# Every 68th quad of edge tiles: its node rows fetched by SyncE, one DMA per edge

## The chip, the core and the metric

The kernel runs on one core of a Trainium2 chip. The core has five instruction streams that run side by side and meet only at semaphores: TensorE (PE; its weight loads are PEld), VectorE (DVE), ScalarE (ACT), GpSimd (POOL) and SyncE (SP). Sixteen DMA engines move data between the chip's memory and the on-chip buffers; SP, ACT and POOL issue the transfers. The metric is the device time of one execution in microseconds, median of several runs; lower is better.

## What is computed

A message-passing layer of a graph network with residual and layer norm. There are 12500 nodes with 160 features (64 scalars `s` and 32 vectors `v` of three components) and 400000 edges, sorted by their destination.

```
h_s = s @ lin1_ws * a / sqrt(64)                 # per node
h_v = v @ lin1_wv * a / sqrt(32)
hid = silu(edge_scalars @ fc_w1 / sqrt(64))      # per edge
w1..w5 = split(hid @ fc_w2 / sqrt(64))
es, ev = h_s[edge_src], h_v[edge_src]            # the gather: one row of 160 floats per edge
messages = products of w1..w5, es, ev and edge_attr
agg  = segment_sum(messages, edge_dst)           # per node
out  = layernorm(x + gate(sc(s, v) + lin2(agg)))
```

## The kernel before

**Stages.** First, the node rows `h_s, h_v` are computed and written to a table `h_tab` in memory, 12500 rows of 160 floats (640 bytes). Then the edges run through a long loop; here almost all the time goes. Node windows that have all their edges are finished inside the loop, the last ones after it.

**The loop.** 128 edges are a tile, four tiles a quad; 3125 tiles make 782 steps of one quad (the last is smaller). The loop is unrolled in the program (`for n, (c, i, tiles) in enumerate(steps)`, line 819). A step:

- `fetch(n + 4)` (line 689): if the step four ahead begins a new chunk of 24 tiles (six steps), SP loads the chunk's edge scalars `es` (`load_chunk`, line 196, two DMAs of 384 KB, two buffers); each 72 tiles (18 steps) SP loads their source indices `idx` and edge attributes `eat` (`ahead`, lines 152 and 153).
- `gather(deep, ...)` (line 448): POOL issues four indirect DMAs, one per tile, each fetching 128 rows of `h_tab` by `idx` into `hg`. The pool `deep` has four buffers of `hg`, so POOL may run up to four quads ahead of the consumer.
- `weights` (line 465): PE forms the edge weights `pw` from `hid`.
- `products` (lines 475 and 483): DVE multiplies `pw` and `hg` to `pr`. This is where a quad's gathered rows are read.
- `select_quad`, `sum_up` (lines 537, 544): a one-hot matrix, scaled by the edge attributes, sums `pr` by destination on PE, two steps later.
- `hide(n + 2)`: PE and ACT compute `hid` for the step two ahead from `es` (lines 443, 445).
- now and then: `output` (second linear maps, register loads of window positions on DVE, line 764, and additions to `acc`), `finish` (a group of 512 nodes: load of `x`, line 592, normalisation, store of the result, line 644), `self_connection` (loads at lines 714 and 716).

**Order.** For PE, DVE, ACT and POOL the order of instructions in the loop is the one written in the program (`manual_schedule`, line 812). SP is not in that list: a scheduler places SP's transfers.

Of the kernel before, what the change touches and what calls it, by code (L numbers as in the profile page):

```python
# [10 lines left out]
F32 = mybir.dt.float32  # L11
I32 = mybir.dt.int32
I16 = mybir.dt.int16
BF16 = mybir.dt.bfloat16
AF = mybir.ActivationFunctionType
OP = mybir.AluOpType
AX = mybir.AxisListType
ENG = mybir.EngineType
PSUM = bass.MemoryType.PSUM

P = 128
# [3 lines left out]
D = S + V3  # L25
# [6 lines left out]
Q = 4  # L32
# [2 lines left out]
CT = 2 * SIDE  # L35
AHEAD = 3 * CT
NF = 4

MARGIN = 128
NO = 16  # L40
# [13 lines left out]
def gnn_kernel(  # L54
# [21 lines left out]
    nc = tc.nc  # L76
    N = x.shape[0]
# [3 lines left out]
    GT = src.shape[2]  # L81
# [7 lines left out]
    h_tab = dram.tile([N, D], F32, name="h_tab")  # L89
# [7 lines left out]
        engines={ENG.PE, ENG.DVE, ENG.Activation, ENG.Pool, ENG.SP}))  # L97
# [33 lines left out]
    steps = []  # L131
# [10 lines left out]
    def ahead(t):  # L142
        a0 = t // AHEAD * AHEAD
        if a0 not in aheads:
            n = min(AHEAD, TT - a0)
            idx = loads.tile([P, AHEAD], I32, name="idx")
            eat = loads.tile([P, AHEAD, 4], F32, name="eat")
            k = 0
            while k < n:
                g, u = divmod(a0 + k, GT)  # L150
                m = min(n - k, GT - u)
                nc.sync.dma_start(idx[:, k:k + m], src[g][:, u:u + m])
                nc.sync.dma_start(eat[:, k:k + m].rearrange("p t k -> p (t k)"),
                                  ea[g].rearrange("p t k -> p (t k)")[:, 4 * u:4 * (u + m)])
                k += m
            aheads[a0] = a0, idx, eat
        return aheads[a0]

    def index(t):
        a0, idx, _ = ahead(t)  # L160
        return idx[:, t - a0:t - a0 + 1]
# [26 lines left out]
    def load_chunk(c, queue=nc.sync):  # L188
        if c in ess:
            return  # L190
        t0, halves = chunks[c]
        es = ess[c] = loads.tile([2 * S, SIDE * P], F32, name="es")
        for half, n in enumerate(halves):
            to = es[half * S:(half + 1) * S]
            e0 = (t0 + half * halves[0]) * P
            queue.dma_start(to[:, :n * P], es_t[:, e0:e0 + n * P])
# [27 lines left out]
    with tc.tile_pool(name="nodes", bufs=len(starts)) as nodes, tc.tile_pool(  # L224
        name="nodes_ps", bufs=6, space=PSUM
# [83 lines left out]
        for c0, cn, quarters, cq, xa, xz in loaded:  # L309
# [6 lines left out]
            for t0 in range(0, nt, U):  # L316
                ps = nps.tile([P, U, P], F32, name="hp")
                for t in range(t0, min(t0 + U, nt)):
                    n = min(P, cn - t * P)
                    nc.tensor.matmul(ps[:n, t - t0], xa[:, t * P:t * P + n], l1,  # L320
                                     start=True, stop=True)
                k = min(U, full - t0)
# [3 lines left out]
                if t0 + k < nt <= t0 + U:  # L326
                    n = cn - full * P
# [6 lines left out]
            for u in range(-(-cq // P)):  # L334
                n = min(P, cq - u * P)
# [10 lines left out]
            if cn > full * P:  # L346
                n = cn - full * P
# [35 lines left out]
    for to, part, pieces, w, r0, c0, by in maps:  # L383
        for k, piece in enumerate(pieces):
# [3 lines left out]
            m = terms.setdefault((to, part, four), len(terms))  # L388
# [45 lines left out]
    def hidden(pool, psum, es, halves, t0, n):  # L434
# [5 lines left out]
        for k, c0, c1 in ((2 * S, 0, ends[1]), (S, ends[1], ends[0])):  # L440
            if c1 > c0:
                c = slice(c0 * P, c1 * P)
                nc.tensor.matmul(ph[:k, c], w1[:k, :k], es[:k, t0 * P + c0 * P:t0 * P + c1 * P],  # L443
                                 start=True, stop=True)
                nc.scalar.activation(hid[:k, c], ph[:k, c], AF.Silu, scale=1.0 / math.sqrt(64))  # L445
        return hid

    def gather(pool, idx):

        hg = pool.tile([P, Q, D], F32, name="hg")  # L450
        for t, i in enumerate(idx):
            nc.gpsimd.indirect_dma_start(  # L452
                out=hg[:, t, :], out_offset=None, in_=h_tab,
                in_offset=bass.IndirectOffsetOnAxis(ap=i, axis=0))
        return hg

    def weights(psum, hid, slots):

        pw = psum.tile([P, Q, 256], F32, name="pw")
        n = len(slots)  # L460
        for t in range(0, n, 2):
            half, c = slots[t]
            m = min(2, n - t)
            assert half == 0 and all(slots[t + k] == (k, c) for k in range(m))
            nc.tensor.matmul(pw[:, t:t + m, :NWT], hid[:m * S, c * P:(c + 1) * P], w2[:m * S, :m],  # L465
                             start=True, stop=True)
        return pw
# [110 lines left out]

    def finish(fin, psum, t0, nt, p, most=NF):

# [27 lines left out]
        def gates():  # L608
            z, sg = held[:2]
            nc.scalar.activation(sg[:, :nt], z[:, :nt, :V3], AF.Sigmoid)  # L610

# [21 lines left out]
        def root():  # L633
            mv, rs = held[4:]
            nc.scalar.activation(rs[:, :nt], mv[:, :nt, 1], AF.Sqrt, bias=eps)  # L635

        def norm():
# [12 lines left out]
    tiles_of_nodes = -(-N // P)  # L650
    LAST = NF
    jobs = [(t, min(NF, tiles_of_nodes - LAST - t), P)
            for t in range(0, tiles_of_nodes - LAST, NF)]
    last_job = (tiles_of_nodes - LAST, LAST, N - (tiles_of_nodes - 1) * P)

    with tc.tile_pool(
        name="fin", bufs=1
    ) as fin, tc.tile_pool(
        name="late", bufs=2
    ) as late, tc.tile_pool(name="edge", bufs=2) as edge, tc.tile_pool(  # L660
        name="deep", bufs=4
# [27 lines left out]
        def fetch(n):  # L689

            if n < len(steps):
                c, i, tiles = steps[n]
                if i == 0:
                    load_chunk(c)
                for t, _, _ in tiles:
                    ahead(t)

        def hide(n):

# [109 lines left out]
                    turning.extend(job[:nt])  # L809
                    doing.extend(job[nt:])  # L810

        with tc.manual_schedule(engines={ENG.PE, ENG.DVE, ENG.Activation, ENG.Pool}):
            fetch(0)
            hide(0)
            waits = []
            pieces = list(range(0, N, CHN))
            products_due = []
            checks = farthest(late)
            for n, (c, i, tiles) in enumerate(steps):
                if 2 <= n < 2 + ZP // 2:  # L820
                    for k in range(2):
                        clear(2 * (n - 2) + k)
                if n in checks:
                    checks[n]()
                fetch(n + 4)
                hg = gather(deep, [index(t) for t, _, _ in tiles])
                pw = weights(pw_ps, hids[c, i // 2], [(half, u - i // 2 * 4) for _, half, u in tiles])

                rest = turning.pop(0)() if turning else None
                step_on = not rest and doing.pop(0) if doing and not turning and not rest else None  # L830
                ready = []

                def first(n=n):
                    if rest:
                        rest()
                    ready.extend(add_up(n))

                oh = one_hot(tiles, pw)
                pr = products(edge, pw, hg, len(tiles), [first, lambda n=n: ready.extend(add_up(n))])
                sel = select_quad(edge, tiles, oh)  # L840
                for a in ready:
                    add(*a)
                if step_on:
                    step_on()
                begin()
                waits.append((tiles, pr, sel))
                if len(waits) > 2:
                    sum_up(n, *waits.pop(0))
                hide(n + 2)
                for blocks, in due(maps_due, n):  # L850
                    output(n, blocks)
                for j, sa in due(turns_due, n):
                    turn_blocks(n, j, sa)
                if products_due:
                    products_due.pop(0)()()
                if n % 30 == 13 and pieces:
                    products_due.extend([lambda: (lambda: None)] * 3 + self_connection(pieces.pop(0)))
            assert not pieces and not products_due
            last_steps = finish(fin, misc_ps, *last_job, most=LAST)
            n = len(steps)  # L860
            while waits:
                sum_up(n, *waits.pop(0))
            while turns_due or maps_due:
                n += 1
                for blocks, in due(maps_due, n):
                    output(n, blocks)
                for j, sa in due(turns_due, n):
                    turn_blocks(n, j, sa)
            assert len(adds) <= NO
            n += 2  # L870
            while adds:
                for a in add_up(n) + add_up(n):
                    add(*a)
            while turning or doing or to_do:
                begin()
                for f in turning:
                    f()()
                for f in doing:
                    f()
                turning.clear()  # L880
                doing.clear()
            for f in last_steps[:LAST]:
                f()()
            for f in last_steps[LAST:]:
                f()
# [4 lines left out]
        with tc.For_i(0, n_redo, 1):  # L890
# [9 lines left out]
            with tc.For_i(0, n_again, 1) as g, tc.For_i(0, GT, 1) as k:  # L900
                t = g * GT + k
# [20 lines left out]
                hg = gather(deep, [idx])  # L922
# [12 lines left out]
                with tc.For_i(first, last + 1, W) as base:  # L935
# [10 lines left out]
                    nc.vector.tensor_scalar_add(r, r, -float(W))  # L946
            for pool, job, most in [(fin, job, NF) for job in jobs] + [(fin, last_job, LAST)]:
                job_steps = finish(pool, misc_ps, *job, most=most)
# [50 lines left out]
```

## Time and profile before

| | |
|---|---|
| median of 3 runs | 4023.07 us (4021.55 to 4029.47) |
| the profiled execution | 4018.78 us |
| its span, first to last instruction | 4017.0 us |
| mean granted clock of TensorE | 0.967 |
| bytes moved by DMA | 411.71 MB, mean 102 GB/s |
| software queue (POOL's transfers) | 27.9% of the 16 engines' span |
| hardware queue of SP | 14.7% |

In the groups of the profile, a row names the line, the engine, the operation and the tiles (out<-in), how often it ran, then after the bar its busy time in us and the mean ns of one, and after the second bar the engine's idle time just before it with what ended most of it. A wait is put down to what came last. SPq, DVEq and so on are the sequencers' own instructions: issues of DMAs, register loads, waits.

SP's longest waits, from the view of waits of the DMA queue (line, what it waited for, us in total, how often, longest):

```profile
SPq L196 <- PE misc L553: 2001.4, 117, 36.0
SPq L152 <- DMA hg<-h_tab,idx: 553.5, 163, 11.9
SPq L714 <- PE misc L720: 261.8, 21, 24.2
SPq L644 <- DVE pw L528: 243.3, 21, 16.4
```

SP spends most of the span waiting until a buffer of `es` or `idx` is free again.

### The profile page before, as it was taken

To read this page: it belongs to the slowest core of one execution; us is meant where nothing else is said; L and a number is where in the kernel's file an instruction comes from. 1 tells how busy PE (TensorE), PEld (TensorE's weight loads), DVE (VectorE), ACT (ScalarE), POOL (GpSimd) and SP (SyncE) were. 2 spreads that over 40 slices of the span, in tenths; PEclk is the share of its full clock that TensorE was granted. 3 is DMA by queue.
4 is the path that set the end of the run, shared out by engine and by line. 5 is a ranking of instruction groups with operands and counts; after the bars stand their busy time and mean duration, and the time that the engine had idled before them with its cause. 6 is when DMAs were issued, how large, how long until landed. Compare 5 with 4: busy or idle time off the path is not lost. (4 is left out here: it accounts for less than half of the span.)

```text
span 4017.0 us, 46675 instructions
## 1 busy us (share of the span) xinstructions
PE 3676.3 (92%) x14291; PEld 1588.0 (40%) x14291; DVE 2410.5 (60%) x6596; ACT 938.7 (23%) x2463; POOL 2982.9 (74%) x3144
## 2 busy tenths in 40 slices
PE   6899899999999999999999999999899989999997
PEld 4344343343343433334333443344343334333443
DVE  5556565655655655656656655666565665655655
ACT  2222222221222222212212222222121221222222
POOL 4777777777777777777777777777777777777775
PEclk8999999999999999999999999999999999999999
DMA  8444444443444444444444444444444444444442
GB/s 240 95 100 98 98 104 96 103 106 94 101 102 98 103 98 102 103 100 101 101 99 100 95 106 101 96 106 99 98 105 95 105 102 95 103 101 98 100 96 58
DMA packets 227691, 411.71 MB, mean 102 GB/s; under 512 B 71883, under 2 KB 157383, under 8 KB 226535
## 3 DMA queue, kind: packets, MB, share of 16 engines
q0 software_dynamic: 152272, 266.53, 27.9%
q1 hardware_dynamic: 74646, 142.01, 14.7%
q8 instruction: 115, 1.88, 0.2%
q14 instruction: 144, 1.18, 0.1%
q10 hardware_dynamic: 514, 0.10, 0.0%
HBM read 392.41 MB, written 16.00 MB: 102 GB/s over the span
## 5 line engine op out<-in xcount | busy, mean ns | idle before, releaser
L452 POOL DMA_INDIRECT hg<-h_tab,idx x3125 | 2968.7, 950 | 962.2 <-issue 865.5
L465 PE MATMUL pw<-w,hid 128*128 128x448 f32 x3126 | 1376.5, 564 | 191.5 <-DVE sel L537 150.1
L544 PE MATMUL pa<-pr,sel 128*64 128x416 f32 x6250 | 1303.5, 539 | 0.0
L475 DVE TENSOR_TENSOR pr<-pw,hg 128x512 f32<-128x512 f32 x782 | 540.5, 691 | 1042.4 <-DMA hg<-h_tab,idx 784.2
L483 DVE TENSOR_TENSOR pr<-pw,hg 128x384 f32<-128x384 f32 x2346 | 1153.6, 547 | 0.0
L465 PEld LDWEIGHTS pw<-w,hid 128*128 128x128 f32 x3126 | 556.3, 195 | 685.8 <-issue 445.3
L544 PEld LDWEIGHTS pa<-pr,sel 128*64 128x64 f32 x6250 | 388.0, 139 | 812.3 <-issue 799.4
L740 ACT COPY sa<-pa 128x416 f32<-128x416 f32 x521 | 263.1, 505 | 1415.4 <-PE pa L544 1413.0
L443 PE MATMUL misc<-es,w 128*128 128x512 f32 (+1 forms) x784 | 448.0, 654 | 17.0 <-DMA es<-in_es_t_dram 14.3
L528 DVE TENSOR_TENSOR pw<-rel,iota 128x64 f32<-128x64 int16 x782 | 178.4, 228 | 468.3 <-PE pw L465 465.5
L445 ACT ACTIVATE hid<-misc 128x512 f32<-128x512 f32 x392 | 233.5, 596 | 743.9 <-PE misc L443 743.4
L553 PEld LDWEIGHTS misc<-ident,sa 128*128 128x128 f32 x2084 | 239.6, 141 | 311.6 <-issue 252.1
L568 PE MATMUL misc<-tt,l 128*96 128x256 f32 (+5 forms) x1496 | 346.0, 378 | 1.7 <-ACT tt L558 1.5
L553 PE MATMUL misc<-ident,sa 128*128 128x128 f32 x2084 | 328.1, 280 | 0.9 <-DVE acc L721 0.8
L537 DVE TENSOR_TENSOR sel<-pw,eas 128x256 f32<-128x256 f32 x782 | 323.6, 414 | 0.0
L556 ACT COPY tt<-misc 128x192 f32<-128x192 f32 x521 | 164.5, 316 | 517.2 <-PE misc L553 516.7
L568 PEld LDWEIGHTS misc<-tt,l 128*96 128x96 f32 (+1 forms) x1496 | 227.0, 162 | 139.6 <-issue 72.6
L443 PEld LDWEIGHTS misc<-es,w 128*128 128x128 f32 x784 | 119.2, 191 | 283.2 <-issue 228.5
L576 DVE TENSOR_TENSOR acc<-acc,os 96x32 f32 x1042 | 195.6, 188 | 23.9 <-ACT os L571 5.5
L603 PE MATMUL misc<-ident,acc 96*128 96x96 f32 x196 | 36.4, 272 | 90.7 <-DVE pw L528 41.8
L558 ACT COPY tt<-misc 128x64 f32<-128x64 f32 x521 | 117.1, 225 | 0.0
L571 ACT COPY os<-misc 96x512 f32<-96x512 f32 (+2 forms) x68 | 38.3, 563 | 303.1 <-PE misc L568 280.4
(84 smaller groups left out, 653.0 us busy)
## 6 DMA issues: line engine op xcount, KB each, us to landing
es<-in_es_t_dram SPq DMA_DIRECT2D x258, 384.0 KB
hg<-h_tab,idx POOLq DMA_INDIRECT x3125
h_tab<-ht POOLq DMA_DIRECT2D x6, 1280.0 KB
xt<-in_x_dram SPq DMA_DIRECT2D x23, 320.0 KB
out_dram<-y SPq DMA_DIRECT2D x23, 320.0 KB
xv<-in_xv_t_dram SPq DMA_DIRECT2D x25, 187.5 KB
xs<-in_xs_t_dram SPq DMA_DIRECT2D x25, 125.0 KB
xa<-in_xs_t_dram SPq DMA_DIRECT2D x6, 512.0 KB
```

The lines of the kernel that those rows point to most:

```text
L443: nc.tensor.matmul(ph[:k, c], w1[:k, :k], es[:k, t0 * P + c0 * P:t0 * P + c1 * P], start=True, stop=True)
L445: nc.scalar.activation(hid[:k, c], ph[:k, c], AF.Silu, scale=1.0 / math.sqrt(64))
L452: nc.gpsimd.indirect_dma_start(out=hg[:, t, :], out_offset=None, in_=h_tab, in_offset=bass.IndirectOffsetOnAxis(ap=i, axis=0))
L465: nc.tensor.matmul(pw[:, t:t + m, :NWT], hid[:m * S, c * P:(c + 1) * P], w2[:m * S, :m], start=True, stop=True)
L475: nc.vector.tensor_mul(two, pw[:, :n, :2 * S].rearrange("p t (k c) -> p t k c", k=2), hg[:, :n, None, :S].to_broadcast([P, n, 2, S]))
L483: nc.vector.tensor_mul(pr[:, :n, first:first + V3].rearrange("p t (i c) -> p t i c", i=3), pw[:, :n, None, 2 * S + k * V:2 * S + (k + 1) * ...
L537: nc.vector.tensor_mul(sel[:, :n], oh[:, :, None, :].to_broadcast([P, n, 4, W]), by_slot(tiles[0][0])[:, u:u + n, :, None].to_broadcast([P ...
L544: nc.tensor.matmul(pa[half * ROWS:(half + 1) * ROWS, :NPR], sel[:, t].rearrange("p k w -> p (k w)"), pr, start=start, stop=stop)
L553: nc.tensor.transpose(pt[:, four * P:four * P + k], sa[:k, c:c + P], ident[:k, :k])
L568: nc.tensor.matmul(po[:, k, :nb], l2[r, terms[to, part, four]], a[:, :nb], start=(n == 0), stop=(n == len(of) - 1))
L576: nc.vector.tensor_add(window, window, os[:, :, b])
L740: nc.scalar.copy(sa, pas.pop(j)[:, :NPR])
```

## The change

Every 68th quad, from step 76 on, is an "own" quad: steps 76, 144, ... 756. For these POOL issues no gather. Instead:

- `places` has SP load the 4 x 128 source indices of the quad into four partitions of a small tile, 74 steps ahead (for the first own quad at step 2).
- 66 steps ahead DVE multiplies them by 640, so that they are byte offsets into the table.
- `rows_of` makes 32 jobs. One job loads 16 offsets into registers of SP and issues 16 DMAs of one row (640 bytes) each, into one partition of `hq`, a tile with a single buffer. From that step on a job is issued in every second step.
- at the own quad, `products` reads `hq` in place of `hg`.
- SP joins the engines whose order in the loop is the written one.

```diff
+OWN = 68
+BATCH = 16
+EVERY = 2
...
+    own = [n for n in range(OWN + 8, len(steps) - 4, OWN) if len(steps[n][2]) == Q]
+    by_bytes = h_tab.rearrange("n d -> (n d)").bitcast(U8)
+    row_bytes = 4 * D
+
+    def places(pool, n):
+
+        at_bytes = pool.tile([Q, P], I32, name="at_bytes")
+        for k, (t, _, _) in enumerate(steps[n][2]):
+            g, u = divmod(t, GT)
+            with nc.allow_non_contiguous_dma(reason="the indices of one tile"):
+                nc.sync.dma_start(at_bytes[k:k + 1], src[g][:, u:u + 1].rearrange("p u -> u p"))
+        return at_bytes
+
+    def rows_of(pool, at_bytes):
+
+        hq = pool.tile([P, Q, D], F32, name="hq", bufs=1)
+        flat_hq = hq.rearrange("p t d -> p (t d)").bitcast(U8)
+
+        def job(t, p0):
+            _, values = nc.values_load_multi_w_load_instructions(
+                at_bytes[t:t + 1, p0:p0 + BATCH], engines=[ENG.SP], min_val=0,
+                max_val=(N - 1) * row_bytes,
+                skip_runtime_bounds_check_because="every entry of src is the index of a node")
+            for p, v in enumerate(values, p0):
+                nc.sync.dma_start(flat_hq[p:p + 1, t * row_bytes:(t + 1) * row_bytes],
+                                  by_bytes[ds(v, row_bytes)][None])
+
+        return hq, [lambda t=t, p0=p0: job(t, p0) for t in range(Q) for p0 in range(0, P, BATCH)]
...
+        name="mine", bufs=2
+    ) as mine, tc.tile_pool(
...
+        at_of, hq_of, rows_due = {}, {}, []
+
+        def fetch_rows(n):
+
+            for m in own:
+                if n == max(1, m - OWN - 6):
+                    at_of[m] = places(mine, m)
+                if n == m - OWN + 2:
+                    nc.vector.tensor_scalar_mul(at_of[m], at_of[m], float(row_bytes))
+                    hq_of[m], jobs = rows_of(mine, at_of[m])
+                    rows_due.extend((m, job) for job in jobs)
+            if n % EVERY == 0 and rows_due:
+                rows_due.pop(0)[1]()
+            assert all(m > n for m, _ in rows_due)
...
-        with tc.manual_schedule(engines={ENG.PE, ENG.DVE, ENG.Activation, ENG.Pool}):
+        with tc.manual_schedule(engines={ENG.PE, ENG.DVE, ENG.Activation, ENG.Pool, ENG.SP}):
...
                 fetch(n + 4)
-                hg = gather(deep, [index(t) for t, _, _ in tiles])
+                fetch_rows(n)
+                hg = hq_of.pop(n) if n in own else gather(deep, [index(t) for t, _, _ in tiles])
```

More of the change, by code (lines that the diff above doesn't have):

```diff
@@ L14 @@
 BF16 = mybir.dt.bfloat16
+U8 = mybir.dt.uint8
 AF = mybir.ActivationFunctionType
```

## The prediction

> **What bounds the kernel now.** I read the busy shares first. PE stands highest, but a busy share names no bound, so I went on to the groups, which say what ended the idle time of each engine.
>
> ```profile
> PE 3676.3 (92%) x14291; PEld 1588.0 (40%) x14291; DVE 2410.5 (60%) x6596; ACT 938.7 (23%) x2463; POOL 2982.9 (74%) x3144
> ...
> L452 POOL DMA_INDIRECT hg<-h_tab,idx x3125 | 2968.7, 950 | 962.2 <-issue 865.5
> ...
> L475 DVE TENSOR_TENSOR pr<-pw,hg 128x512 f32<-128x512 f32 x782 | 540.5, 691 | 1042.4 <-DMA hg<-h_tab,idx 784.2
> ```
>
> POOL's gathers take 0.95 us each, and what precedes them is "issue": POOL waits for nothing but itself. DVE, at the first product of a quad, waits 784 us in all for gathered rows. The timeline of POOL near the end shows it closely:
>
> ```profile
> 3956.09 0.95 POOL L452 DMA_INDIRECT hg<-h_tab,idx  x1 [0.30 <-issue]
> 3957.35 0.95 POOL L452 DMA_INDIRECT hg<-h_tab,idx  x1 [0.30 <-issue]
> 3958.60 0.95 POOL L452 DMA_INDIRECT hg<-h_tab,idx  x1 [0.30 <-issue]
> ```
>
> That is one gather per 1.25 us, the 0.30 us between two included. The line's own answer puts the first gather at 65.4 us and the last at 3984.9: 3919.5 / 3124 = 1.2547 us each, without a pause over the whole span. So POOL bounds, at 4 x 1.2547 = 5.02 us a step, 65 us in and 32 us out. PE follows, with room as the table of stretches shows (PE's busy time is the second number):
>
> ```profile
> 1000.00:2000.00 1000.00, 927.27 (x3580) 395.76 (x3579) 607.30 (x1678) 237.79 (x626) 756.99 (x798) 0.98 0.43 101
> 2000.00:3000.00 1000.00, 926.03 (x3554) 395.33 (x3554) 598.68 (x1642) 230.34 (x616) 757.21 (x798) 0.97 0.42 100
> ```
>
> PE is idle 73 us in 1000, and the DMA engines are 43% busy. The profiled execution took 4018.78 us (span 4017.0), 4.3 below the median of 4023.07; I work in the profiled time and add 4 at the end.
>
> **What is removed.** Own quads are steps 76, 144, ... 756: eleven, with 44 gathers. 44 x 1.2547 = 55.2 us leave POOL. The gain holds only if the others can use it: each time POOL gets 5.0 us ahead, the consumers must make that up before the next own quad, 68 steps (341 us) later. PE's idle time there is 0.073 x 341 = 25 us, so 5 are to be had; after the last one 25 steps (125 us, 9 idle) remain. POOL may run ahead because `deep` has four buffers and an own quad uses none. I take the full 55.
>
> **What is added, off SP.** Eleven multiplications of 4x128 integers on DVE (the nearest row, pw<-rel at 128x64, took 0.23 us): under 4 us in all, under DVE's 39% idle. DMA load: 5632 rows of 640 bytes are the bytes that the gathers moved before. 44 loads of one tile's indices. All nothing, since DMA is 43% busy and POOL's pace does not follow it; if that cover went, a gather's landing would come later by some tenths of a us, once.
>
> **What is added on SP** decides. Per own quad there are 32 jobs, each one register load of 16 values and 16 DMAs that follow one another. SP's rows before:
>
> ```profile
> 68.23 0.31 SPq L391 DMA_DIRECT2D l<-in_lin_ws_dram  x1
> 68.59 1.82 SPq L391 DMA_DIRECT2D l<-in_lin_wv_dram  x4
> 70.45 0.42 SPq L391 DMA_DIRECT2D l<-in_lin_ws_dram  x1
> 70.91 1.81 SPq L391 DMA_DIRECT2D l<-in_lin_wv_dram  x4
> 72.77 0.42 SPq L391 DMA_DIRECT2D l<-in_lin_ws_dram  x1
> 73.23 1.81 SPq L391 DMA_DIRECT2D l<-in_lin_wv_dram  x4
> 75.09 1.11 SPq L196 DMA_DIRECT2D es<-in_es_t_dram  x2
> ...
> L764 DVEq TENSOR_LOAD <-rows x68: 536/1099/2294, 153.2 to 3998.5; - x68
> L889 SPq TENSOR_LOAD <-redo x1: 476/476/476, 195.9 to 195.9; - x1
> L889 DVEq TENSOR_LOAD <-redo x1: 310/310/310, 4007.8 to 4007.8; - x1
> ```
>
> *One DMA, c.* Small ones back to back come every (75.09 - 68.59) / 14 = 0.464 us; one alone takes 0.31, and with the 0.045 between two makes 0.355. No row has an address from a register. The far upper row is es (64 partitions of 6 KB, median 0.530, so 0.575 with the gap). A row here is one run on one partition; the one-partition load of dst (L282) took 0.462 to issue. I take 0.464, because two near rows agree on it; the ends 0.355 and 0.575 stay.
>
> *One register load, L.* DVE's queue took 0.310 for one value and 1.10 for its usual 16: (1.10 - 0.31) / 15 = 0.053 a value. SP's single value took 0.476; 0.476 + 15 x 0.053 = 1.27, with a gap 1.31.
>
> *The rest of SP in 68 steps:* 11 es pairs x 1.16, 4 idx and eat loads of about 1.6, x, out, xs and xv about 4, indices 2: 25 us. After an es pair the queue can stall, since the compiled order has every DMA of SP wait for the one eight before it, and the pair lands late: issued at 2007.0, it kept the DMA engines over 0.9 busy until 2013.0. A load and eight rows take 1.31 + 8 x 0.464 = 5.0 after the pair's own 1.1, that is 6.1 against 6.0; I put 0.7 a pair, 8. The last row's landing, 2. Together 35.
>
> *The sum and its limit.* T = 32 x (16c + 1.31) + 35 = 32 x 8.73 + 35 = 314 us. The jobs start once DVE has passed the products of the own quad before (one buffer, `bufs=1`) and the multiplication two steps on; the rows are due 68 steps after that quad, of which POOL issues 67: 336.3 - 2 x 5 = 326. 314 fits, with 12 to spare. Beyond 326 each us is paid in full eleven times; at 331 the 5.0 gained are gone. By c: full gain to 0.485, break-even at 0.496.
>
> SP's other work now stands in the program's order, no longer chosen by the scheduler. Queued behind a waiting row are es (used two steps after its place, 10 us, for 6 of landing), idx (POOL wants it about 2.5 steps on) and the output stores. While T is under 326 SP arrives at each in time; I cost it at nothing, and at up to 25 us if idx comes late for POOL some ten times.
>
> One rule of the Trainium skill speaks against the change: "Runtime: NRT & Kernel Launch", section "Instruction fetch mechanics", puts a register load at about 200 ns for each register even in bulk. The 16 values of L764 at 1.10 us contradict it. By it a load would be an estimated 3.2 us, T = 32 x (7.42 + 3.2 + 0.05) + 35 = 376, 50 late, and the time 4018.78 - 55 + 550 + 4 = 4518 instead of the sum below.
>
> **The rivals.**
> *SP keeps up (chance 0.50).* 4018.78 - 55.2 + 4.3 = 3967.9, say 3968; by itself 3960 to 3985.
> *SP is too slow for the rows (0.39).* An address from a register or the stalls behind es bring c over 0.496. DVE then waits at each own quad for hq, and POOL soon for its four buffers. At c = 0.53 (es's median, no gap): T = 32 x 9.79 + 35 = 348, 22 late, 4018.8 - 55 + 242 + 4 = 4210. At 0.575: T = 371, 45 late, 4463. For it: only 6% between my c and the limit, and no register address in the trace. Against it: one run instead of 32 per DMA, and rows alone at 0.31.
> *Half the gain (0.06).* POOL stalls on late indices, or the consumers recover only part: 3968 + 27 = 3995.
> *No net change (0.05).* T lands between 329 and 332, so that waiting for hq eats the 5 us: about 4022.
> That the change does not do what it says is out: the compiled POOL program has 44 gathers fewer, and SP's has 5632 row DMAs.
>
> **How the numbers follow.** About 0.2% (8 us) is what a measurement here can tell from none. Faster: 0.50 + 0.06 = 0.56; same 0.05; slower 0.39. The predicted time is the first case's, 3968. The range goes down to 3955 (a little more than POOL's share, from steadier feeding) and up to 4300, which is c = 0.545 (T = 356, 30 late: 4018.8 - 55 + 330 + 4 = 4298); what lies above is c from there on, about 0.15. The forecast's own range is 3960 to 3985.
>
> **What would show it.** In the trace after: row DMAs on SP spaced by about 0.46 us and loads of about 1.3; 3081 gathers still 1.25 apart; DVE's wait for hg smaller by some tens of us and none to speak of for hq. Wrong if DVE shows waits of 10 us or more for hq eleven times, or SP's spacing is over 0.50, or POOL's gathers show pauses before own quads.

## The result, and the profile after

| | before | after |
|---|---|---|
| median, same chip, 4 runs each | 4022.82 us | 3977.84 us (3976.66 to 3978.59) |
| profiled execution | 4018.78 us | 3976.66 us |
| its span | 4017.0 us | 3974.7 us |
| granted clock of TensorE | 0.967 | 0.968 |

The ratio is 0.988, with an interval of 0.9869 to 0.9892: the change makes the kernel 45 us faster. The forecast was 3968, that is 0.9863 of the median shown before; its sign, its mechanism and its own range (3960 to 3985) held, its size was some 10 us too favourable.

The page of the changed kernel, two of its groups:

```profile
L456 POOL DMA_INDIRECT hg<-h_tab,idx x3081 | 2938.5, 954 | 945.3 <-issue 852.6
...
L508 DVE TENSOR_TENSOR pr<-pw,hg 128x512 f32<-128x512 f32 x771 | 532.6, 691 | 914.4 <-DMA hg<-h_tab,idx 656.8
```

POOL issues 44 gathers fewer and still waits mostly for itself ("issue"); DVE still waits for gathered rows, 127 us less than before. The bound is the same engine with less to do. A gather takes 954 ns in the mean here instead of 950; how much of that belongs to the change is taken up with e3.

What stands in place of those gathers, from the views of the tile `hq` and of the line that loads the registers (count, then shortest, median and longest in ns, then first and last start in us):

```profile
L485 SPq MOVE hq<-h_tab x5632: 29/29/42, 118.4 to 3797.4; - x195
L485 SPq DMA_DIRECT2D hq<-h_tab x5632: 219/228/307, 118.4 to 3797.4; - x195
L508 DVE TENSOR_TENSOR pr<-pw,hq x11: 691/692/693, 448.6 to 3820.2; 128x512 f32<-128x512 f32 x11
its engine sat idle before it (us, times) until:
  DVE pw L561: 0.7, 4
```

```profile
L480 SPq TENSOR_LOAD <-at_bytes x352: 984/1231/1896, 117.1 to 3790.1; - x176
```

DVE never waits for `hq`: what little idle time precedes its eleven reads is charged to its own earlier work. A row costs SP 0.228 us for the DMA and 0.029 for setting its address, and with the gaps the timeline gives the whole step:

```profile
414.27 7.10 SPq L485 DMA_DIRECT2D hq<-h_tab  x16
...
425.50 11.56 SPq L485 DMA_DIRECT2D hq<-h_tab  x32
```

The 32 rows with one register load among them take 11.56 us; less 1.28 for the load and the gap behind it that is about 0.32 us a row. Row after row starts mostly 0.320 to 0.323 us apart in the records. These are the last rows of the first own quad, whose product begins at 448.6: they are issued 11 us early. Over the eleven own quads the margin lies between 10 and 41 us.

The span can be split by the gathers alone: the time to the first, the spacing to the last, and what follows the last.

| profiled execution | first gather | gathers | mean spacing | last gather to end | span |
|---|---|---|---|---|---|
| before | 65.4 | 3125 | 1.2546 | 32.1 | 4017.0 |
| after | 60.5 | 3081 | 1.2587 | 37.5 | 3974.7 |

So of the 42.3 us, 55.2 come from the 44 gathers and 4.9 from an earlier start; 3080 x 0.00403 = 12.4 are given back by a slower stream and 5.4 at the end. Nearly all of the 12.4 is in the length of the gathers, not between them: no pause of POOL after its first gather is longer than 0.4 us. The experiments ask where these terms come from, and whether the place and the price of the slower case were right.

The end has one plain part, the records of the program's last line:

```profile
L1046 POOLq DRAIN  x3: 46/103/7908, 3965.9 to 3974.4; - x3
L1046 SPq DRAIN  x3: 7/7/13, 3969.3 to 3974.1; - x3
```

and the same line of the kernel before:

```profile
L995 POOLq DRAIN  x3: 46/103/2845, 4012.8 to 4016.7; - x3
L995 SPq DRAIN  x3: 7/7/13, 4016.1 to 4016.4; - x3
```

Before, POOL's last drain (2.845 us from 4012.8) was over at 4015.6 while SP still had to end at 4016.1: it was free. After, it takes 7.908 us from 3965.9 to 3973.8, and SP is done at 3969.3. The program ends 0.9 us behind SP's drain before; after, 5.4 us behind it. That is 4.5 us that the change pays at its end.

### The profile page after: what moved, and what is told of

Same layout as the page of the kernel before. It is cut to its first block, busy times and chain, and to the rows that moved or that the text cites. A ratio compares the mean times of both kernels' runs of the same rounds, so it can differ in the third digit from the quotient of the medians.

```text
span 3974.7 us, 58310 instructions
## 1 busy us (share of the span) xinstructions
PE 3659.0 (92%) x14291; PEld 1589.7 (40%) x14291; DVE 2416.5 (61%) x6607; ACT 940.7 (24%) x2463; POOL 2952.7 (74%) x3100
## 5 line engine op out<-in xcount | busy, mean ns | idle before, releaser
L456 POOL DMA_INDIRECT hg<-h_tab,idx x3081 | 2938.5, 954 | 945.3 <-issue 852.6
L516 DVE TENSOR_TENSOR pr<-pw,hg 128x384 f32<-128x384 f32 x2313 | 1136.1, 546 | 0.0
L447 PEld LDWEIGHTS misc<-es,w 128*128 128x128 f32 x784 | 118.7, 191 | 286.7 <-issue 227.1
```

Source lines behind the costliest of these rows:

```text
L456: nc.gpsimd.indirect_dma_start(out=hg[:, t, :], out_offset=None, in_=h_tab, in_offset=bass.IndirectOffsetOnAxis(ap=i, axis=0))
L516: nc.vector.tensor_mul(pr[:, :n, first:first + V3].rearrange("p t (i c) -> p t i c", i=3), pw[:, :n, None, 2 * S + k * V:2 * S + (k + 1) * ...
```

## The experiments

The runs e1 to e7 were made on two chips on which the kernel before took 4019.8 and 4019.6 us. The other five ran on two chips on which the kernel before itself took 5171 and 5109 us and TensorE was granted a clock of 0.82 to 0.88; those are compared among themselves only.

**e1: the order of SP alone.** The kernel before, with SP in the list of engines whose order is the written one.

```diff
-        with tc.manual_schedule(engines={ENG.PE, ENG.DVE, ENG.Activation, ENG.Pool}):
+        with tc.manual_schedule(engines={ENG.PE, ENG.DVE, ENG.Activation, ENG.Pool, ENG.SP}):
```

> The kernel before with one line of the change: SP joins the engines in the written order; no own quads. In the trace after, POOL's first gather starts 4.9 us earlier (60.5 instead of 65.4) and its gathers come every 1.2587 us instead of 1.2547, 12 us in all. Theory A (the row transfers slow POOL's gathers): 4023 - 5 = 4018, gathers 1.2547 apart. Theory B (SP's written order slows them, because its loads and stores now fall elsewhere): 4018 + 12 = 4030, gathers 1.2587 apart. Theory C (they slow down when the consumers run closer behind): 4018, as A.

Measured 4019.93 us, ratio 0.9999 (0.999 to 1.0008). First gather at 61.2, spacing (3984.6 - 61.2) / 3124 = 1.2559, 33.6 us behind the last. So the earlier start goes with the written order: in the trace SP no longer loads `xs`, `xv` and further `idx` and `eat` just before its last store to the table, and POOL's waits ahead of its first gather end at 59.6 in the changed kernel instead of 64.5. In this execution the stream is 3.9 us slower (2.5 of it are four pauses of about 1 us) and the end 1.5 us longer: together nothing. That the gain came from the order is refuted.

**e2: rows and gathers both.** POOL gathers the own quads too, into a tile that nobody reads.

```diff
-                hg = hq_of.pop(n) if n in own else gather(deep, [index(t) for t, _, _ in tiles])
+                hg = gather(deep, [index(t) for t, _, _ in tiles])
+                hg = hq_of.pop(n) if n in own else hg
```

> The whole change, but POOL gathers the own quads as well; products still read hq. All of the change's cost, none of its gain. Theory A: 4023 - 5 + 12 = 4030, gathers 1.2587 apart. Theory C: about 4018, 1.2547 apart. Theory B: 4030, and then e1 also. If SP's rows were late anywhere, over 4040.

Measured 4037.96 us, ratio 1.0039 (1.0025 to 1.0053), 18 us slower than before. Without the saved gathers nothing of the gain is left; that much is clear. But the 18 us are not the price of the rows. The waits of POOL show what is in them:

```profile
POOL hg L456 <- issue: 856.2, 2808, 0.3
POOL hg L456 <- DMA hg<-h_tab,idx: 47.4, 102, 3.6
```

In the changed kernel the longest wait of the second kind is 0.3 us; here seven pauses of about 2.4 to 3.6 follow an own quad's unread gather. A tile without a reader comes free only when its own rows have landed, so these pauses belong to the experiment. Of the rest, some 6 us are longer gathers (2974.8 us busy against 2968.7).

**e3: no rows.** The change without index loads, register loads and rows.

```diff
+        hq_once = mine.tile([P, Q, D], F32, name="hq", bufs=1)
+        nc.vector.memset(hq_once, 1.0)
...
-                fetch_rows(n)
-                hg = hq_of.pop(n) if n in own else gather(deep, [index(t) for t, _, _ in tiles])
+                hg = hq_once if n in own else gather(deep, [index(t) for t, _, _ in tiles])
```

> The change without index loads, offsets, register loads and rows: the own quads read a tile that was filled once, so the rows of these 44 tiles are left out of the result. The gain without the cost. Theory A: 4023 - 5 - 55 = 3963, gathers 1.2547 apart. Theory C: 3975, since the own quads still let POOL run ahead and the consumers catch up. Theory B: 3975, and then e1 slow as well.

Measured 3966.96 us, ratio 0.9864 (0.9848 to 0.9879): 52.9 us, 8 more than the change. Spacing (3929.0 - 61.0) / 3080 = 1.2558 as in e1; the stream of the changed kernel is 8.7 us slower than that. It would be natural to put these 8.7 us down to the rows, but the gathers themselves do not bear it out:

```profile
L456 POOL DMA_INDIRECT hg<-h_tab,idx x3081 | 2929.5, 951 | 945.4 <-issue 847.5
```

Without rows a gather takes 951 ns. It also takes 951 in e4 (the same rows), in e6 (a quarter more) and in e7 (three quarters more); only the profiled execution of the change has 954. So no price of the rows per gather is shown. That the change is 8 us slower than e3 is the likeliest size and not a proof, since the intervals overlap by a little, and where these 8 us sit differs from one profiled execution to the next. The consumers did keep up with all that POOL saved.

**e4: the rows with SP left to the scheduler.**

```diff
-        with tc.manual_schedule(engines={ENG.PE, ENG.DVE, ENG.Activation, ENG.Pool, ENG.SP}):
+        with tc.manual_schedule(engines={ENG.PE, ENG.DVE, ENG.Activation, ENG.Pool}):
```

> The change with SP left to the scheduler. If the written order is worth what the head shows, 3978 + 5 = 3983. If the scheduler puts the 5632 rows ahead of loads of es and idx that are due earlier, or the other way round, there are waits at own quads: 4050 and more.

Measured 3974.89 us, ratio 0.9888 (0.9873 to 0.9903), the same as the change and not the 3983 expected. First gather at 66.2, spacing 1.2562. Against before, the stream is 3080 x (1.2562 - 1.2546) = 5 us slower here, with the rows and without the written order; against e3, which has no rows, it is 1 us slower. Single profiled executions fix what the rows take from the stream no closer than 1 to 9 us.

**e5: more own quads.** One in 52, fetched in batches of 32 every third step.

```diff
-OWN = 68
-BATCH = 16
-EVERY = 2
+OWN = 52
+BATCH = 32
+EVERY = 3
```

> Every 52nd quad is an own quad (14 instead of 11), in 16 jobs of one load of 32 registers and 32 rows, every third step. With the measured 0.323 us a row and 0.05 us a register above 0.48 for a load, T = 16 x (32 x 0.323 + 2.1) + 25 + 16 = 240 us against a limit of 51 x 5.02 - 10 = 246. If the limit holds as the prediction put it: no waits for hq, 12 more gathers gone, 3978 - 15 = 3963. If SP needs more room than the sum says: waits at the own quads, 3978 or slower.

Measured 3968.53 us, ratio 0.987 (0.9853 to 0.9886): 51 us, where 56 gathers are worth 70. The interval overlaps that of the change, so it is not shown to be better. The page shows a part of where the rest went:

```profile
L456 POOL DMA_INDIRECT hg<-h_tab,idx x3069 | 2919.0, 951 | 963.4 <-issue 851.7
```

POOL is idle 963.4 us before 3069 gathers; at the changed kernel's 0.3068 a gather it would be 942, so 22 us are new. In the records they are nine pauses, and six of these, 16 us, stand before the first gather that uses a new load of `idx` (steps 126, 198, 270, 486, 594 and 685; a load serves 18 steps). The longest, in the timeline:

```profile
2455.86 10.73 SPq L485 DMA_DIRECT2D hq<-h_tab  x32
...
2466.69 1.13 SPq L200 DMA_DIRECT2D es<-in_es_t_dram  x2
...
2468.12 0.38 SPq L156 DMA_DIRECT2D idx<-in_src_dram  x1
...
2474.10 0.95 POOL L456 DMA_INDIRECT hg<-h_tab,idx  x1 [5.19 <-DMA hq<-h_tab]
```

SP issues a job of 32 rows, then the `es` loads, and `idx` only after them; POOL's gather starts 6.0 us after that issue. The label names rows of `hq`, which a gather does not read; they are what landed last by the profile. In all six cases the gather starts 5.7 to 7.2 us after SP issued the load; at the 37 loads without a pause it is 7.1 to 42 us. So it is mainly late `idx` that stops POOL here, in the case shown behind a long row job. Only two pauses, 4 us together, follow an own quad by five steps and end with DVE's products: there POOL has run ahead into full buffers. The profiled execution is the slowest of the four, 8 us above the median, so the others may have fewer such pauses.

**e6 and e7: a longer queue of SP.** Each job issues 4, or 12, more rows, into a spare tile.

```diff
+        spare = pool.tile([P, D], F32, name="spare", bufs=1)
+        flat_spare = spare.bitcast(U8)
...
+                if p < p0 + 4:
+                    nc.sync.dma_start(flat_spare[p:p + 1],
+                                      by_bytes[ds(v, row_bytes)][None])
```

> The change with four more row transfers in every job, into a spare tile that nobody reads. SP's work per own quad becomes 249 + 32 x 4 x 0.323 = 290 us, under the limit of 326. By the prediction's step: no change, 3978. If the rows' traffic slows POOL's gathers in proportion (theory A): 12 x 0.25 = 3 us more, 3981.

> The same with twelve more in every job: 249 + 32 x 12 x 0.323 = 373 us, 47 over the limit of 326. By the step of the slower rival: DVE waits for hq at every own quad, 11 x 47 = 517 us, so 3978 + 517 = 4495. If SP's lateness is absorbed elsewhere (POOL's four buffers, the 10 us at the start): under 4300.

e6 measured 3977.98 us, ratio 0.9895 (0.9878 to 0.9911): 1408 rows more cost nothing that can be measured. So SP has room, as the sum with 0.323 us a row says, and the bulk of rows by itself does not press on the gathers in proportion. Its trace has a first sign of what comes next: two pauses of POOL, 4 us together, at new loads of `idx`.

e7 measured 4573.55 us, ratio 1.138 (1.1361 to 1.1399), 596 us over the change where 517 were expected. The cliff is there, near its place and in full for every own quad. But what is late is not what the expectation, and the prediction's second case, named. Waits of PE in e7:

```profile
PE misc L447 <- DMA es<-in_es_t_dram: 740.5, 109, 15.5
```

its reads of the tile `hq`:

```profile
  DMA hq<-h_tab: 37.9, 6
```

and the longest of POOL's waits for anything but itself:

```profile
POOL hg L456 <- DMA hq<-h_tab: 337.2, 39, 14.5
```

PE waits 740 us for the edge scalars, DVE 38 us for the own rows. The 337 us of POOL under the name of `hq` are late `idx` again: at 40 of the 43 changes to a new load of `idx` POOL stands before the first gather that uses it, 361 of its 602 us of pauses, and the gather starts 5.1 to 6.9 us after SP issued the load. In SP's written order the loads of `es` and `idx` stand between the row jobs; when a job takes longer than its two steps, each load behind it is late, PE and POOL stand still, and DVE with them. The own rows are hardly late because the loop itself has been slowed to SP's pace: from one own quad's product to the next it takes 385 to 406 us, against 334 to 340 in the changed kernel. The 79 us beyond the sum stay unexplained; PE also ran at a granted clock of 0.911 here against 0.967 in e6.

**e8 to e12: on the two other chips.** e8 is e6 with 8 extra rows, e9 fetches only the first eight own quads, e10 and e12 fetch half of a quad every 30 steps, e11 is the change again. The edits of e9 and of e10 (its main lines):

```diff
-    own = [n for n in range(OWN + 8, len(steps) - 4, OWN) if len(steps[n][2]) == Q]
+    own = [n for n in range(OWN + 8, len(steps) - 4, OWN) if len(steps[n][2]) == Q][:8]
```

```diff
+OWN = 30
+BATCH = 32
+EVERY = 3
+H = 2
...
-                hg = hq_of.pop(n) if n in own else gather(deep, [index(t) for t, _, _ in tiles])
+                ids = [index(t) for t, _, _ in tiles]
+                hg = gather(None, ids, hq_of.pop(n), H) if n in own else gather(deep, ids)
```

> The change with eight more row transfers in every job: 249 + 32 x 8 x 0.323 = 332 us of SP's work per own quad, 6 over the limit of 326. By the step of the prediction: 11 x 6 = 66 us more than the change, 3978 + 66 = 4044. If the limit is softer, because SP starts ahead or the buffers absorb it: 3980. If late loads of es cost before the limit is reached: over 4100.

> The change with the first eight own quads alone: 3093 gathers. Gathers alone: 12 x 1.2547 = 15 us back, 3978 + 15 = 3993. If POOL's drain at the very end (2.845 us with 3125 gathers, 7.908 with 3081, in all runs so far) goes with the number of gathers and not with the presence of row transfers, it has a value of its own here, and what is not 7.908 shows in the tail.

> Own halves instead of own quads: every 30th step SP brings the first two tiles of the quad, in 8 jobs of 32 rows, and POOL gathers the other two into the same tile; 25 halves, 50 gathers fewer. SP's work per half is 120 us of 29 x 5.02 - 10 = 136. If what held e5 back was POOL running 5 us ahead into full buffers, steps of 2.5 us are taken whole: 3978 - 6 x 1.2547 = 3970, and 5 less if rows cost as in the change. If the consumers' pace is the limit: no better than the change, 3978.

> The changed kernel again, on the same chip as e10, for the comparison: 3978 by its earlier runs, 45 less than the kernel before.

> The kernel of e10 once more (two tiles of a quad by SyncE every 30 quads, 32 rows a job, a job every third step: 25 half quads, 50 gathers fewer), on a chip where the kernel before takes about 4020 us. If the gain follows the number of gathers while POOL bounds: -50 x 1.2559 = -62.8, head -4, POOL's final drain about +4.6 (on the disturbed chip it took 7.418 us with these 3075 gathers, 2.845 with 3125), row traffic of the change scaled by 50/44 +7: about -55, 3965, ratio 0.986. If POOL running ahead more often than the consumers can follow limits it, as in e5: -45 to -50, 3970 to 3975. If SyncE's load sets the end (25 x 8 jobs of 32 rows, 8 x 3 steps = 24 steps of 5.05 us for 256 x 0.323 + 8 x 2.1 = 100 us, so 121 against 100): not expected; the time would then be over 4000 and POOL would show pauses before the half quads.

| | median us | ratio to before on the same chip | interval |
|---|---|---|---|
| e8, 8 extra rows a job | 6215.24 | 1.2006 | 1.195 to 1.2062 |
| e9, eight own quads | 5314.92 | 1.0255 | 1.0198 to 1.0313 |
| e10, halves | 5556.3 | 1.0728 | 1.0685 to 1.077 |
| e11, the change | 5332.93 | 1.0295 | 1.0257 to 1.0333 |
| e12, halves, another chip | 5474.68 | 1.0718 | 1.0678 to 1.0758 |

The expectations of times do not apply, since they were made for POOL as the bound: e9, e10 and e11 missed outright, and where e8 and e12 named a slower case (over 4100, over 4000) the kernel before already lies above it. The waits of POOL in e11:

```profile
POOL hg L456 <- DVE pr L516: 1265.7, 267, 15.0
```

and of DVE and ACT in e11:

```profile
DVE pw L561 <- remote: 1400.4, 163, 15.3
...
ACT sa L790 <- remote: 575.5, 64, 19.3
```

POOL waits 1266 us for its consumers, and ACT and DVE stop again and again, up to 19 us at a time, for something that the profile shows on no engine of this core ("remote"). With POOL waiting for others a saved gather has nothing to save, and the change costs 3%. What stops ACT and DVE, and through what the change lengthens it, stays open. So do the place of the threshold between 4 and 12 extra rows and the halves as a better version: neither was tried on a chip where POOL is the bound. In e8 PE does wait 1035 us for `es`, in e11 on the same chip 44, so eight extra rows a job already make `es` late there. In e12 the halves do show a weakness of their own: PE waits 280.8 us for `es` and POOL 174.4 us for `idx`, so batches of 32 rows every third step are long enough to hold up SP's other loads.

These runs do give one thing that is the same on all these chips, POOL's last drain:

| gathers | 3069 | 3075 | 3081 | 3093 | 3125 |
|---|---|---|---|---|---|
| kernels | e5 | e10, e12 | after, e3, e4, e6, e7, e8, e11 | e9 | before, e1, e2 |
| drain, us | 6.928 | 7.418 | 7.908 | 8.888 | 2.845 |

Every kernel with the same number of gathers has the same drain, to the nanosecond, with rows (after) or without (e3), with rows and all gathers (e2) or with neither (e1). Between 3069 and 3093 it grows by 1.960 / 24 = 0.0817 us a gather; by that 3125 would give 11.50, and it has 2.845, so somewhere between it falls back.

## Why the prediction was right, point by point

**The bound and what is removed: right.** 44 gathers at 1.2547 are 55.2 us, and e3 brought 52.9 in the medians. The consumers made up what POOL gained: in the step after an own quad DVE reads its rows 7.0 us (mean of eleven) after POOL's last gather for them ended, against a median of 2.3 in the kernel before, and 20 steps on it is 2.4 again, well inside the 68 there are. With 56 gathers saved (e5) two pauses of 2 us at full buffers appear.

**The cost on SP: right in sign, wrong in its main term.** c was put at 0.464 us a row, "because two near rows agree on it"; it measured 0.323, below even the lower end of 0.355. The two do not agree on one thing: 0.464 is the spacing of SP's loads of weights, while the 0.462 of L282 is the issue alone, without the gap to a next one, and of a load that ACT's queue issued. One contiguous row of 640 bytes to one partition, its address in a register, is cheaper than each of them, and the address itself costs only a 0.029 us move. The register load was well sized (1.31 with its gap; measured 1.23 + 0.05). By the Trainium skill ("Runtime: NRT & Kernel Launch", "Instruction fetch mechanics") a load would have been an estimated 3.2 us for its 16 registers; that section speaks of register I/O that the runtime adds, the values here lie in an on-chip tile, and for these the 1.231 us of this case's trace decides. No run here shows the page's own case.

The stall behind `es` was put at 8 us for each own quad. The waits of SP's queue, changed kernel:

```profile
SPq L677 <- DVE pw L561: 564.8, 21, 48.7
SPq L480 <- DVE pw L561: 227.1, 8, 35.0
SPq L485 <- DMA es<-in_es_t_dram: 172.4, 144, 2.6
```

The third line is that stall: 172.4 / 11 = 16 us, twice the estimate. With both, T = 32 x (16 x 0.323 + 1.28) + 25 + 16 + 2 = 249 us instead of 314, against the limit of 326. The 77 us of room are about what SP waits at the output stores (first line) and at the first job of an own quad (second line): (564.8 + 227.1) / 11 = 72. So the 0.39 for "SP is too slow" rested on a price 44% too high. That case's size came near: e7 took T by the same sum to 249 + 32 x 12 x 0.323 = 373, 47 late, and paid 54 us at each of eleven own quads. Three slips in the working change nothing: 3919.5 / 3124 is 1.2546, by the sum the full gain reaches to c = 0.4865 and not 0.485, and from 0.464 to the limit of 0.496 it is 7%.

**The place of the slower case: wrong.** "DVE then waits at each own quad for hq" was the mechanism; e7 shows PE waiting for `es` (740 us) and POOL for `idx` (361 us), DVE for `hq` 38 us. The step that failed is the one that costed SP's written order: it named what is queued behind a row job (`es`, `idx`, the output stores), found them in time as long as T is under 326, put a price on a late `idx` only, and let the rows be what is late beyond. T under 326 is not enough either: in e6 (T = 290) and in e5 (240 against its own limit of 246) `idx` comes late for POOL now and then, since a load waits for what stands ahead of it in SP's queue, whatever the sum over 68 steps.

**Half the gain, and no net change: did not come.** `idx` holds up nothing in the profiled execution of the changed kernel, though the closest gather starts 6.2 us after the issue of its `idx`, and in e5 gathers at 5.7 to 7.2 us are the ones with pauses. The mechanism of "half the gain", POOL stalled on late indices, was the right thing to fear: it is most of what e5 shows.

**What was not in the sum.** In the profiled execution the missing 13 us are -4.9 at the start, +12.4 in the stream and +5.4 at the end. The earlier start goes with the written order (e1, e3) and is given back: e3's stream, without any row, is 3.7 us slower than before as well. At the end POOL's last drain loses its cover, 4.5 us; e3 has the same drain, so this comes with the fewer gathers and not with the rows. The rest of the stream, 8.7 us, is longer gathers in this one execution (954 ns where e3, e4, e6 and e7 have 951), and what lengthened them stays open. "DMA is 43% busy and POOL's pace does not follow it" agrees with e4, e6 and e7. That the measured time lies within 3960 to 3985 although these terms were missing, and although c and the stall behind `es` were both off, in opposite directions, is in part luck: the upper end of that range was not worked out from any of them.

**The signs named beforehand.** Loads of about 1.3 and no wait for `hq`: as said. Rows at 0.46: 0.323. Gathers "still 1.25 apart": 1.2587. DVE's wait smaller by some tens of us: by 127.

## What to carry to other kernels

Where one engine's instruction stream sets the pace, moving some of its work to an engine that mostly waits can be worth the moved instructions almost in full (52.9 of 55 us in e3, 45 with the cost of the change), as long as the consumers have idle time to follow; ask how long the borrowed engine's own queue becomes ahead of each of its regular loads, for these are late first and not the new work. The price of an instruction that no trace shows should keep its whole range until one run measures it: here one row cost 0.323 us, below even the 0.355 to 0.575 that the nearest rows said. When a wait is put down to a tile that the waiting instruction does not read, look at which step it falls on. Split the span into start, stream and end before summing; the two edges moved by 5 us each here, and neither was in the sum.

## What the runs showed of the hardware that was not expected

- A DMA of one 640-byte row with its address in a register leaves SP mostly every 0.320 to 0.323 us; its issue took 0.228 us in the median of 5632, and 0.307 at most.
- POOL's last drain goes with the number of gathers alone in the fourteen traces, by 0.0817 us for each from 3069 to 3093, and falls back somewhere between 3093 and 3125; why is not shown. A kernel with a few gathers more or fewer can be several us longer at its end for that.
- The same kernel took 4020 us on some chips and 5110 to 5170 us on two others; on one of these the change that gains 1.2% elsewhere loses 3%.
- A load that SP issues behind a job of 32 rows (10.7 us of issue) held POOL for up to 5.2 us in e5, and the profile put that wait down to the rows.
